# Folding layer norm's sums and the last pairs' key sums with accumulating transfers in a two-layer attention kernel

## The chip, the cores and the metric

The kernel runs on one core of a Trainium2 chip. The metric is the device time of one execution in microseconds (us): 2938.17 before the change, the median of three runs (2936.75 to 2938.68). The profile is of one execution, with a span of 2935.6 us at a mean granted TensorE clock of 0.997.

## The reference

The input x has 8 images of 512 channels and 32 x 32 = 1024 positions, float32. Two attention layers follow each other. Layer 0 normalises each position over its 512 channels, has 8 heads of 64 and adds x. Layer 1 normalises groups of channels and has one head of 512. Cut to what matters:

```python
def _L0_conv_ref(x, Wq, bq, Wk, bk, Wv, bv, Wo, bo, gamma, beta):
    x_flat = x.reshape(B, C, S).transpose(0, 2, 1)
    xn = layer_norm(x_flat, gamma, beta)        # mean and variance over the 512 channels
    q, k, v = ...                               # xn @ W.T + b, 8 heads of 64
    attn = softmax(q k^T / 8)
    return (attn v) @ Wo.T + bo + x_flat

def _L1_conv_ref(x, gamma, beta, wq, bq, wk, bk, wv, bv, wp, bp):
    h = _group_norm(x, gamma, beta)             # 32 groups
    q, k, v = ...                               # w h + b
    attn = softmax(q^T k / sqrt(512))
    return x + wp (v attn^T) + bp
```

So each image needs two sums over channels for each position in layer 0 (of x, and of the squares of x minus its mean), and for each head and query the sum of the exponentials over the keys.

## The kernel before, in words

**Tiling.** Channels or keys lie on the 128 partitions, positions on the free axis. A big tile holds 128 x 1024 float32 (46 of them in one pool), a half tile 128 x 512 (9 of them). A tile of x is a "block": two groups of 128 channels by 512 positions, so that one image is four blocks `xt[j, k]`, j the half of the channels and k the half of the positions. PSUM has three wide tiles (two banks each) and two single banks.

**Products.** Every projection is a blocked product in seven multiplications rather than eight (class `Product`, the list `STEPS`). One step multiplies one block of the left by one block of the right, into an accumulating bank called x, y or z. Some operands are sums of blocks, which VectorE makes: for the right operand they are called T1 to T4 (T1 = 12 - 11, T2 = 22 - T1, T3 = 22 - 12, T4 = 21 - T2), for the left S1 to S4. The third step of a product multiplies S2 and T2. A product is two units (four for layer 1's scores) of seven steps. After its matmuls a step first performs one "tick", then ScalarE or VectorE takes a bank out: a copy `u`, then sums with another bank (line 343).

**Order.** Within `manual_schedule` each engine performs its instructions in the order of the text. Work that may be done beside the matmuls stands in a queue, `side`; a tick performs its first entry, `later(...)` appends, and `until(...)` empties it until a condition holds. Entries of `at_scores` are performed after the fifth score tile of the next pair.

**Layer 0's norm.** `LayerNorm.steps` is a generator whose pieces go through `side`, one at a tick. It adds the blocks of x on VectorE (`lns`, lines 524 and 528), multiplies the sum by a matrix of 1/512 on TensorE (`over_channels`, line 519), which gives the means on 64 partitions of a bank, and has ScalarE copy them to the four quarters of `mu` (line 537). It centres x, squares it on ScalarE, adds the squares (`lnq`) and multiplies again for the variance. `compact` takes 16 columns out of the transposed bank, `inverse_root` finds the root, and `expand` spreads it over a whole tile. The blocks are then scaled. The norm of image b + 1 is queued in `next_values_and_queries`, after the third step of image b's values.

**Layer 0's heads.** A `Pair` is two heads and 512 queries; there are eight for each image. For each of eight blocks of keys TensorE makes scores (line 683), ScalarE the exponentials (line 686), and VectorE adds them up over the blocks (line 692). What is left is a sum over 128 partitions: 64 x 2 keys for each head. For pairs 0 to 5 transfers issued by GpSimd do most of this. `halve` adds the upper 64 partitions to the lower (line 716), `fold` lays 32 partitions over another 32 into a quarter of a half tile (line 713), and `folded_sums` transposes 32 x 32 squares and reduces on VectorE. For pairs 6 and 7 a matmul with ones does it (`product`, line 749), and the last pair's output is multiplied by the inverse sums as it leaves its bank (line 708). The output blocks of those pairs are block 22 of `ot`.

**Layer 1.** `Whole` holds its scores, exponentials, key sums (also folded, in `Whole.fold`) and values. `values` is a product of two units with eight matmul instructions of 512 columns a step; its order is two steps of each unit, then the rest of the first, then the rest of the second. After it come the next image's values and queries.

**What is around.** Loads and stores are issued by SyncE in the order of the text. Weights were saved to DRAM once and are reloaded for each image (`load_w`), and the next image's keys come back as `k_again`.

## Time and profile before

| what | value |
|---|---|
| time, median of 3 | 2938.17 us |
| span of the profile | 2935.6 us, 26956 instructions |
| s matmuls (line 683) and acc matmuls (line 701), busy | 457.1 and 453.6 us |
| ScalarE exponentials (line 686) | 512 of 1050 ns |
| VectorE additions of exponentials (line 692) | 384 of 1225 ns |
| mean matmuls (line 519) | 32 in 8 images, 9.4 us busy |
| variance matmuls (line 519) | 32 in 8 images, 10.6 us busy |
| key sum matmuls of the last pairs (line 749) | 64 in 8 images, 8.5 us busy |
| halving transfers (line 716) | 64 of 256 KB, 3.4 to 7.6 us to landing, median 3.5 |
| folding transfers (line 713) | 256 of 64 KB, 1.8 to 7.4 us to landing, median 2.4 |
| loads of x (line 150) | 32 of 512 KB, 5.3 to 6.8 us to landing, median 6.0 |

A line of the page's groups gives line, engine, operation, output and input tiles with their shapes and count, then busy time and mean duration, then the idle time of the engine before it and what ended it. In a timeline the first number is the start, the second the time from there to the end of the row's last instruction. A float32 matmul of the text appears as two instructions. Matmuls are pipelined, so that the distance of two starts tells what one costs, and its duration is longer.

### The profile page before, as it was taken

How to read it: one execution, taken by the hardware profiler on the slowest of the kernel's cores; microseconds unless marked ns; L12 is line 12 of the kernel's file. 1: busy time of each engine (PE TensorE's matmuls, PEld its weight loads, DVE VectorE, ACT ScalarE, POOL GpSimd, SP SyncE). 2: the span in 40 equal slices, each digit the busy share in tenths (PEclk: the TensorE clock that was granted, in tenths of full speed). 3: DMA queues.
4: the chain of work that ended last, by engine and by line, in shares of the span. 5: the costliest groups of instructions: out<-in, count | busy, mean ns of one | idle time of the engine just before them, and what ended most of it. 6: DMA issues, size and time to landing. Idle time of an engine off the chain costs nothing.

```text
span 2935.6 us, 26956 instructions
## 1 busy us (share of the span) xinstructions
PE 2914.7 (99%) x9787; PEld 1374.3 (47%) x9787; DVE 1788.5 (61%) x2298; ACT 1044.1 (36%) x1641; POOL 238.5 (8%) x357
## 2 busy tenths in 40 slices
PE   9999999999999999999999999999999999999998
PEld 4534455345543455434553345533455334553344
DVE  6677456774567654675557765577555675537744
ACT  3462215612156121651216512264223632226221
POOL 2020000200011000110001100011000100002000
PEclk9999999999999999999999999999999999999999
DMA  8124141231312323132232322322231231412302
GB/s 296 59 47 146 53 136 35 58 138 55 125 39 55 136 66 113 43 83 104 69 111 47 83 101 77 103 52 78 100 112 68 58 107 65 122 33 63 109 4 70
DMA packets 100286, 250.93 MB, mean 85 GB/s; under 512 B 13824, under 2 KB 17968, under 8 KB 100144
## 3 DMA queue, kind: packets, MB, share of 16 engines
q1 hardware_dynamic: 81616, 204.51, 20.4%
q0 software_dynamic: 18432, 44.59, 7.7%
q8 instruction: 79, 1.29, 0.2%
q14 instruction: 63, 0.52, 0.1%
q10 hardware_dynamic: 96, 0.02, 0.0%
HBM read 156.26 MB, written 59.24 MB: 73 GB/s over the span
## 4 chain that ended last, share of the span: by engine, by line
PE 98%; DVE 1%; DMA 0%; issue 0%; ACT 0%; SPq 0%; DVEq 0%
PE s L683 15%; PE acc L701 15%; PE x_o L429 6%; PE x_s L421 6%; PE y_s L421 4%; PE y_o L429 4%; PE z_s L421 4%; PE z_o L429 4%; PE x_q L404 3%; PE x_k L404 3%; PE x_qa L404 3%; PE x_v L413 3%; PE x_vm L413 3%; PE x_out L404 3%; PE y_q L404 2%; PE z_qa L404 2%
## 5 line engine op out<-in xcount | busy, mean ns | idle before, releaser
L686 ACT ACTIVATE p<-s 128x1024 f32<-128x1024 f32 x512 | 476.4, 1050 | 77.3 <-PE s L683 77.2
L692 DVE TENSOR_TENSOR sum<-sum,p 128x1024 f32<-128x1024 f32 x384 | 470.3, 1225 | 38.9 <-ACT p L686 0.9
L701 PE MATMUL acc<-p,v 128*64 128x512 f32 x2048 | 453.6, 595 | 0.0
L683 PE MATMUL s<-q,k_again 64*128 64x512 f32 x1792 | 399.9, 596 | 0.0
L701 PEld LDWEIGHTS acc<-p,v 128*64 128x64 f32 x2048 | 141.4, 137 | 305.0 <-issue 292.2
L683 PEld LDWEIGHTS s<-q,k_again 64*128 64x128 f32 x1792 | 166.3, 185 | 232.0 <-issue 116.1
L716 POOL DMA_DIRECT2D sum<-sum x64 | 54.9, 859 | 2294.9 <-PE z_vm L413 1139.3
L713 POOL DMA_DIRECT2D fold<-sum x256 | 171.2, 764 | 292.5 <-DMA fold<-sum 281.6
L690 DVE TENSOR_TENSOR sum<-p,p 128x1024 f32<-128x1024 f32 x64 | 78.4, 1225 | 190.0 <-ACT p L686 190.0
L421 PE MATMUL x_s<-S_qa,T_gn 128*128 128x512 f32 x256 | 120.3, 592 | 0.0
L429 PE MATMUL x_o<-T_p,S_vm 128*128 128x512 f32 x256 | 115.2, 592 | 0.0
L822 ACT ACTIVATE p<-p 128x512 f32<-128x512 f32 x128 | 80.7, 630 | 73.1 <-DVE p L343 73.1
L705 ACT COPY o<-acc 128x512 f32<-128x512 f32 x56 | 32.8, 586 | 197.4 <-PE acc L701 197.4
L343 DVE TENSOR_TENSOR p<-u(1, 1)_s,y_s 128x512 f32<-128x512 f32 x32 | 22.0, 689 | 132.3 <-ACT u(1, 1)_s L434 132.3
L451 ACT ACTIVATE u(0, 0)_k<-x_k,vecs 128x512 f32<-128x512 f32 x16 | 11.0, 687 | 239.7 <-PE x_k L404 211.0
L343 DVE TENSOR_TENSOR y<-u(1, 1)_o,y_o 128x512 f32<-128x512 f32 x16 | 11.0, 688 | 134.7 <-ACT u(1, 1)_o L434 134.7
L421 PEld LDWEIGHTS x_s<-S_qa,T_gn 128*128 128x128 f32 x256 | 48.6, 190 | 61.2 <-issue 61.0
L429 PEld LDWEIGHTS x_o<-T_p,S_vm 128*128 128x128 f32 x256 | 48.6, 190 | 60.7 <-issue 60.7
L758 ACT COPY rr<-r 32x16 f32<-32x16 f32 x256 | 51.6, 202 | 58.2 <-DVE r L657 55.3
L496 DVE STREAM_TRANSPOSE rden<-rr 128x512 f32<-128x512 f32 (+1 forms) x72 | 51.5, 750 | 26.1 <-ACT rr L878 13.4
L343 DVE TENSOR_TENSOR qa<-u(1, 1)_qa,y_qa 128x512 f32<-128x512 f32 x16 | 11.0, 687 | 82.4 <-ACT u(1, 1)_qa L451 82.4
L413 PE MATMUL x_vm<-w_m,T_gn 128*128 128x256 f32 x256 | 60.5, 379 | 0.0
(327 smaller groups left out, 4541.8 us busy)
## 6 DMA issues: line engine op xcount, KB each, us to landing
x<-in_x_dram SPq DMA_DIRECT2D x32, 512.0 KB, 6.0
sum<-sum POOLq DMA_DIRECT2D x64, 256.0 KB, 3.5
fold<-sum POOLq DMA_DIRECT2D x256, 64.0 KB, 2.4
xr<-in_x_dram SPq DMA_DIRECT2D x64, 256.0 KB, 6.8
x_away<-x SPq DMA_DIRECT2D x32, 512.0 KB
x1r<-x_away SPq DMA_DIRECT2D x64, 256.0 KB, 5.9
out_dram<-y SPq DMA_DIRECT2D x64, 256.0 KB, 2.5
k_away<-k SPq DMA_DIRECT2D x28, 512.0 KB, 2.6
```

Source lines behind the costliest of these rows:

```text
L404: nc.tensor.matmul(dst, a[:, k, ts(r, P)], b[:, k, :], start=(opens and k == 0), stop=(k == 1), skip_group_check=True)
L413: nc.tensor.matmul(dst[:, ts(m, CB)], b[:, k, ts(2 * r + m, P)], a[:, k, :], start=(opens and m == 0 and k == 0), stop=(k == 1), skip_grou ...
L421: nc.tensor.matmul(dst, b[:, k, ts(r, P)], a[:, k, :], start=(opens and k == 0), stop=(k == 1), skip_group_check=True)
L429: nc.tensor.matmul(dst, a[:, m, ts(r, P)], b[m // 2][:, m % 2, :], start=(opens and m == 0), stop=(m == NM // 2 - 1), skip_group_check=True)
L683: nc.tensor.matmul(s[:, ts(i, HB)], self.k[m // 4][r, ts(m % 4, P)], self.q[r, :], start=True, stop=True)
L686: nc.scalar.activation(p, s, AF.Exp, scale=1.0 / float(D) ** 0.5)
L690: nc.vector.tensor_add(self.sum, self.p[0], p)
L692: nc.vector.tensor_add(self.sum, self.sum, p)
L701: nc.tensor.matmul(acc[i * D : (i + 1) * D, :], value_of(self.vt, m, self.c * P + i * D, D), self.p[m][:, ts(i, HB)], start=(m == 0), stop ...
L713: nc.gpsimd.dma_start(out=f[ts(q, BL), :], in_=t[ts(n, BL), cols], accum_op=ALU.add if n else ALU.bypass)
L716: nc.gpsimd.dma_start(out=t[:D, :], in_=t[D:, :], accum_op=ALU.add)
L822: nc.scalar.activation(dest(i, k), dest(i, k), AF.Exp, scale=float(C) ** -0.5)
```

## The change

The aim is to take sums over partitions off TensorE and to let transfers that add do them.

1. **Means.** For images 1 to 7 the sum over channel groups is made by four transfers from DRAM into one tile, the first plain and three adding, issued by GpSimd (`LayerNorm.sums`). `halve` and `fold` follow, and VectorE's `folded_sums` gives the sums, which are spread with eight small ScalarE copies and one transpose (`folded_means`, `spread`). For image b + 2 these sums are issued while image b is at layer 1's values; for image 1 they are issued before image 0's keys.
2. **Variances.** The sum of squares is still added on VectorE, then halved and folded in the same way. Because a transfer takes time, the norm waits between (`waiting`) until the next image's queries begin.
3. **Last pairs.** Pairs 6 and 7 are folded like the others in all images but the last. Their inversion goes through `side` behind three empty entries, and pair 7's output is copied out and scaled afterwards like that of pair 6.
4. **Folds.** A pair's sum is halved and folded as soon as its scores are through (`take`), before the values of the pair ahead, and both first parts of a fold are issued before the two adding parts.
5. **Order.** The norm of image b + 2 is queued within layer 1's values, with x loaded there; the weights of the queries are loaded after them; the query product has one tick a step instead of two.

```diff
-LN_AT = 3
...
+    def fold(f, q, t):
+
+        for n in range(2):
+            for i in range(NH):
+                nc.gpsimd.dma_start(out=f[ts(q + i, BL), :], in_=t[ts(n, BL), ts(i, HB)],
+                                    accum_op=ALU.add if n else ALU.bypass)
...
     class LayerNorm:
...
+        def sums(self):
+
+            self.total = big_tile(f"lns_{self.b}")
+            for c in range(NC):
+                nc.gpsimd.dma_start(out=self.total, in_=x[self.b, ts(c, P), :],
+                                    accum_op=ALU.add if c else ALU.bypass)
+            self.fold("mu")
...
+        def fold(self, name):
+            self.f = half_tile(f"fold_{name}_{self.b}")
+            halve(self.total)
+            fold(self.f, 0, self.total)
+
+        def folded_means(self, name):
+
+            d = small.tile([P, HB // BL], F32, tag=f"ln{name}", name=f"ln{name}_{self.b}")
+            t = half_tile(f"fold{name}_{self.b}")
+            folded_sums(d[:D, :], t[:D, :], self.f[:D, :])
+            nc.vector.tensor_scalar(d[:D, :], d[:D, :], 1.0 / C, None, ALU.mult)
+            return d
+
+        def spread(self, name, r):
+            rr = small.tile([P, NH, HB // BL], F32, tag=f"ln{name}r", name=f"ln{name}r_{self.b}")
+            for j in range(4):
+                for k in range(NH):
+                    nc.scalar.copy(rr[ts(j, BL), k, :], r[ts(k, BL), :])
+            yield
+            t = big_tile(f"{name}_{self.b}")
+            setattr(self, name, t)
+            expand(t, rr.rearrange("p k i -> p (k i)"))
+            yield
...
         def steps(self):
...
-            for k in range(NH):
-                yield from self.add("lns", k, self.xt[0, k], self.xt[1, k])
-            yield
-            self.mean()
-            yield
-            yield
+            if self.folded:
+                yield from self.spread("mu", self.folded_means("m"))
+            else:
...
-            yield
-            self.variance()
-            yield
-            yield from self.root()
+            if self.folded:
+                self.fold("var")
+                yield
+                while self.waiting:
+                    yield
+                yield from self.root_folded()
+            else:
...
+        def take(self, pair):
+
+            n = len(self.two)
+            self.two.append(pair)
+            if self.folded:
+                if n == 0:
+                    self.f = half_tile(f"fold_{self.tag}")
                 halve(pair.sum)
-            for n, pair in enumerate(self.two):
-                for i in range(2):
-                    fold(self.f, 2 * n + i, pair.sum, ts(i, HB))
+                fold(self.f, 2 * n, pair.sum)
...
+        ln = LayerNorm(1)
+        ln.sums()
+        ln.xt = load_x(1)
         units, kt = project("k0", wk_now, bias_of("bk0"), hb)
...
             units, q = project(f"q{b}", wq, bias_of("bq0"), hb, True)
-            for u in units:
-                u.pieces = 2
+            units[0].step(0 if b else 6)
+            if ln:
+                ln.waiting = False
             units[0].rest()
...
-                p.values(scaled=(p is pairs[-1]))
...
+                p.values(scaled=(i == HEADS - 1 and not more))
+                sums = groups[i // 2]
...
+                elif i % 2 == 1 and sums.folded:
+                    if i + 1 < HEADS:
+                        at_scores.append(sums.invert_folded)
                     else:
-                        sums.product()
-                        later(sums.invert, sums.copies, lambda: sums.rows(1), lambda: sums.rows(0),
-                              lambda: sums.scale(0))
-                elif i + 1 < len(pairs):
-                    at_scores.append(sums.invert_folded)
+                        later(*(nothing,) * 3, sums.invert_folded)
                     later(sums.copies, *(lambda s=sums, f=f, n=n: f(s, n) for f in (PairSums.rows, PairSums.scale)
                                          for n in range(2)))
...
             if more:
-                wv_next, wq_next = load_w("v", b + 1), load_w("q", b + 1)
+                wv_next = load_w("v", b + 1)
             o_units = whole.values(vm)
             check = iter(()) if more else all_checks()
             o_units[0].step(1)
+            ln = LayerNorm(b + 2) if b + 2 < B else None
+            if ln:
+                ln.sums()
             whole.inverse()
             o_units[0].step(1)
             next(check, None)
             o_units[1].step(2)
             next(check, None)
-            for u in o_units:
-                u.rest()
-            until(lambda: not side)
+            o_units[0].rest()
+            if ln:
+                ln.xt = load_x(b + 2)
+                ln.queue()
+            o_units[1].rest()
+            if more:
+                wq_next = load_w("q", b + 1)
```

## The prediction

> **What bounds the kernel now.** I read the page from its head: busy time, the clock in the slices, the chain that ended last.

> ```profile
> PE 2914.7 (99%) x9787; PEld 1374.3 (47%) x9787; DVE 1788.5 (61%) x2298; ACT 1044.1 (36%) x1641; POOL 238.5 (8%) x357
> PEclk9999999999999999999999999999999999999999
> PE 98%; DVE 1%; DMA 0%; issue 0%; ACT 0%; SPq 0%; DVEq 0%
> ```

> TensorE is busy in all but 21 us of 2935.6, at full clock, and the chain is made of it. So a matmul taken out of its queue is time taken off the end, unless another engine then makes TensorE wait. Next, what TensorE waited for: 13 us in all, nearly all single waits at the kernel's start and in its last image. No stage repeats a wait, so little can be gained from waits; the price list is what each removed matmul takes in the stream. The timeline of TensorE round the mean, the variance and the last pairs' key sums, for the fifth image's norm and for the fourth image's last pairs:

> ```profile
> 1524.76 1.89 PE L413 MATMUL z_v<-w_v,x 128*128 128x256 f32 x8
> 1526.58 1.08 PE L519 MATMUL mean<-lns,ones_c 128*64 128x512 f32 x4
> 1527.59 1.99 PE L413 MATMUL x_v<-w_v,T_h 128*128 128x256 f32 x8
> 1529.42 1.89 PE L413 MATMUL y_v<-w_v,T_h 128*128 128x256 f32 x8
> ...
> 1541.48 1.88 PE L404 MATMUL y_q<-T_h,w_q 128*128 128x512 f32 x4
> 1543.29 1.08 PE L519 MATMUL var<-lnq,ones_c 128*64 128x512 f32 x4
> 1544.30 1.98 PE L404 MATMUL x_q<-T_h,w_q 128*128 128x512 f32 x4
> 1546.12 1.88 PE L404 MATMUL z_q<-T_h,w_q 128*128 128x512 f32 x4
> ...
> 1309.50 1.07 PE L749 MATMUL den<-sum,ones 128*32 128x512 f32 x8
> 1310.50 7.09 PE L701 MATMUL acc<-p,v 128*64 128x512 f32 x32
> ```

> Durations overlap, so I take starts. A step of v follows the next at 1.73 us (y_v to the following x_v: 1531.15 - 1529.42), so two steps should take 3.45; from z_v to y_v it is 4.66: the mean costs 1.21 us. For q a step is 1.72, two 3.43; from y_q to z_q 4.64: the variance costs 1.21. The key sums cost 1310.50 - 1309.50 = 1.00.

> [...] (512 KB weight saves land in 3.1 us at the fastest) [...] 256 KB add in 3.5. [...] 281.6 us of idle time before the fold transfers end with a fold landing. [...]

> **Part 1, off TensorE.** Images 1 to 7 lose mean and variance matmuls, images 0 to 6 the last pairs' product: 7 x (1.21 + 1.21 + 1.00) = 23.9 us, all on the path. Image 0's norm and image 7's product stay.

> **Part 2, the last pairs' scaling.** Their fold starts when pair 7's sum is done. Before, that sum ended at 1309.4. Halving 3.8 (3.5 and the wait) and two rounds of folds, 3.2 each, give 1319.8; the inversion now comes at the k projection's fourth step, after VectorE's addition ends at 1322.4 (1321.4 with TensorE 1.0 earlier). Hidden, by 1.6 us, behind k's first unit. But scale(0) and scale(1) now fall into the ticks of out's first two steps, which pushes T1 and T2 of o back by a tick. The same stage before:

> ```profile
> 1331.60 0.75 DVE L783 SCALAR_TENSOR_TENSOR u(0, 0)_out<-x_out,bo,xr 128x512 f32<-128x512 f32 x1 [1.03 <-PE x_out L404]
> 1332.27 1.22 DVE L483 TENSOR_TENSOR T_o<-o,o 128x1024 f32<-128x1024 f32 x1
> 1333.40 0.68 DVE L343 TENSOR_TENSOR x<-u(0, 0)_out,z_out 128x512 f32<-128x512 f32 x1
> 1334.00 1.22 DVE L483 TENSOR_TENSOR T_o<-o,T_o 128x1024 f32<-128x1024 f32 x1
> 1335.14 0.75 DVE L783 SCALAR_TENSOR_TENSOR u(0, 0)_out<-x_out,bo,xr 128x512 f32<-128x512 f32 x1
> ```

> With the new order a scaling (0.69) stands where T1 stood at 1332.27, T1 where T2 stood at 1334.00, and T2 comes after the x_out addition of the second unit, at 1335.80, and ends at 1336.95. TensorE wants T2 for its fifth out step, which started at 1336.55: a stall of 0.5 us, 7 times, **+3.5 us**. Bounds: none (0), or a whole tick (1.7 us, 12 in all).

> **Part 3, sums of x from DRAM.** Per image 1 to 7: four 512 KB transfers into one tile, chained; one halving; four folds in two rounds. No row shows a 512 KB add. From above: 3.1 us (a plain save) at the least, 7.6 (the slowest halving) at the most. The estimate: from 64 KB (2.4) to 256 KB (3.5) is 1.1 us for 192 KB, so 512 KB is 5.0; with wait and issue 5.3. Chain: 4 x 5.3 + 3.8 + 6.4 (two rounds of folds) = 31.4 us.

> When does it start? In the loop it is issued after the first two steps of layer 1's values in the text, but GpSimd runs ahead: its last fold for layer 1's key sums was issued at 1460.5, and the new order of these folds is no longer. The tile needs a free big buffer; the last to come free is one of the value projection's operands, at 1462.9. I take 1462: the sums are ready at 1493.4.

> When are they needed? At the tick of the second value unit's third step. VectorE gets there when the first unit's last addition ends, 1496.2. So no wait on a DMA, with 2.8 us in hand. Then VectorE: transpose 0.7, reduce 0.7, multiply 0.2, to 1497.8. ScalarE: eight copies (1.7, as the pairs' eight do), to 1499.5; queued behind them, the copy u(0, 1) of that step, 0.6, to 1500.2. TensorE wants it for the fifth step, which started at 1500.65. It just fits: +0.

> VectorE beside it: the two wide and two half additions of x go (2 x 1.22 + 2 x 0.69 = 3.8 us per image), transpose, reduce and the spread of the mean (1.25) come (2.9). The centring moves up into the last value steps and delays the next v additions by some 2 us; the banks that they free are wanted later than that. No cost. ScalarE loses four 0.58 copies. Nothing here is on the path.

> **Part 4, variances.** Halve and fold, 10.2 us, after the last sum of squares: the seventh tick of v's first unit, about 1522.5, so ready at 1533; read at q's first step, 1535. Hidden, behind v's second unit. Image 1: the sums start at about 40 us, beside the loads of the start, and are read at 86: hidden, though the saves of the weights queue behind them and free their buffers 15 to 20 us later.

> **Part 5, moved loads.** x, 2 MB, now issued at 1496.7 and landing 6 us later (6.0 median), before the centring that follows two ticks after the mean; w_q after the last store, 1513.7, for use at 1536. Hidden. The traffic grows by 7 x 2.1 MB = 15 MB on 251, at DMA shares of 1 to 4 tenths.

> Sum: -23.9 + 3.5 = -20.4; 2938.2 - 20.4 = 2917.8.

> **The rivals.**
> A, the forecast: 2918, with T2's stall; spread 2914 to 2921. Chance 0.58.
> B, the delayed T2 costs nothing, because the scalings run in gaps of VectorE: 2938.2 - 23.9 = 2914. For it: VectorE is 61% busy. Against: the listing shows VectorE without a gap of 0.1 us from 1331.6 to the end of T2. 0.10.
> C, the means come late. VectorE waits in its queue, ScalarE's copies behind it, and TensorE for u(0, 1). With 7.6 + 0.3 us a transfer the chain is 31.6 + 3.8 + 6.4 = 41.8, to 1503.8; plus 1.6 + 1.7 + 0.6 = 1507.7, against 1500.65: 7 us in each of six images, 42 in all: 2960, slower. Against: few loads run in that window once x and w_q are moved. For: a margin of 2.8 us is thin, and the adding rate from DRAM is not shown. 0.23, of which 0.06 still gain 6 us or more, 0.06 land within 6 us of before and 0.11 are slower.
> D, buffers: in the first image saves and sums share GpSimd's queue and x takes four tiles early; a fold's tile is held longer in the pool of nine half tiles. One or two stalls, 2 to 10 us: 2920 to 2928. 0.09.

> **How the numbers follow.** Faster by over 0.2% (5.9 us): A, B, D and a quarter of C, 0.83. Same: 0.06. Slower: 0.11. The range leaves out C's far side and the edges: from B's 2914 less 2 us for waits that vanish too, to 2930, the mild side of C.

> **What would show it.** TensorE's instructions fall by 7 x (4 + 4 + 8) = 112 to 9675; line 519's matmuls remain 8 in all, the key sum product 8. TensorE waits 7 times some 0.5 us for T_o. If the means are in time, VectorE's transpose of the folded means waits for no DMA; if rival C holds, it waits for "fold" and TensorE for ScalarE's u(0, 1)_o, in six places. A time over 2932 would mean that some wait of 2 us or more per image took the matmuls' place; one under 2912 that a removed matmul cost more than its slot.

## The result and the profile after

The changed kernel takes 2947.74 us (median of 4) beside 2937.6 of the kernel before (median of 4, a fourth run beside the three known before): ratio 1.0035, 95% interval 1.0018 to 1.0052. It is slower by 10 us, where 20 us less were forecast.

The page of the changed kernel, in the order in which the one before was read: busy time, clock, chain. PE is TensorE and PEld its loading of weights, DVE is VectorE, ACT ScalarE, POOL GpSimd and SP SyncE; a q behind the name stands for the engine's instruction queue.

```profile
PE 2901.9 (98%) x9675; PEld 1374.4 (47%) x9675; DVE 1790.7 (61%) x2307; ACT 1054.5 (36%) x1732; POOL 363.1 (12%) x525
PEclk9999999999999999999999999999999999999999
PE 85%; DVE 6%; DMA 5%; ACT 2%; issue 2%; POOL 0%; SPq 0%; DVEq 0%; POOLq 0%; ACTq 0%
```

112 matmul instructions are gone, as forecast. But TensorE's idle time rose from 20.9 to 45.6 us, and the chain is no longer TensorE alone: 13% of it is VectorE, transfers and ScalarE. What TensorE waited for, in the view of waits (us in total, times, longest), cut to what is new:

```profile
PE y_k L403 <- DVE k L342: 17.2, 7, 2.7
...
PE x_q L403 <- ACT u(0, 1)_q L450: 3.5, 7, 1.1
...
PE x_out L403 <- DVE T_o L482: 1.9, 7, 0.3
PE y_v L412 <- DVE v L342: 1.3, 4, 0.3
```

One wait stands out: once for each of images 0 to 6, the last step of the next k projection's first unit waits about 2.5 us for VectorE. That is the sign that the prediction named for a time over 2932, a wait of 2 us or more per image in the matmuls' place. The timeline of TensorE there, for the fourth image; a bracket gives the engine's idle time before the row and what ended it:

```profile
1328.34 1.88 PE L403 MATMUL x_k<-T_h,w_k 128*128 128x512 f32 x4
1330.06 1.88 PE L403 MATMUL z_k<-T_h,w_k 128*128 128x512 f32 x4
1334.61 3.18 PE L403 MATMUL y_k<-x,w_k 128*128 128x512 f32 x4 [2.67 <-DVE k L342]
1337.58 2.43 PE L403 MATMUL x_out<-o,w_o 128*128 128x512 f32 x4
1339.84 1.88 PE L403 MATMUL z_out<-o,w_o 128*128 128x512 f32 x4
```

A step's row lasts 1.88 us and the next starts 1.72 after it (x_k to z_k). So from z_k to z_out, three steps, it should be 5.15 us; it is 9.78. The wait is only part of it: y_k and x_out are themselves slow. The busy times by stretch show why. A row gives the stretch, its length and the busy time and instructions of PE, PEld, DVE, ACT and POOL; then come the granted clock, the DMA engines' share and GB/s:

```profile
1330.00:1334.60 4.60, 1.94 (x5) 0.57 (x3) 2.19 (x7) 2.88 (x10) 0.00 (x0) 1.00 0.18 57
1334.60:1336.00 1.40, 1.39 (x3) 0.64 (x4) 1.40 (x3) 0.00 (x0) 0.00 (x0) 0.73 0.21 57
1336.00:1338.00 2.00, 2.00 (x4) 0.89 (x3) 0.54 (x2) 0.00 (x0) 0.00 (x0) 0.50 0.24 91
1338.00:1340.00 2.00, 2.00 (x5) 0.85 (x4) 1.12 (x2) 0.00 (x0) 0.00 (x0) 0.83 0.00 0
```

After the wait the clock is halved for 3.4 us (in the trace's clock record from 1335.26 to 1338.67); the 40 slices of the page, each 74 us long, don't show it. Over the seven images the excess from z_k to z_out is 4.34, 2.58, 4.25, 4.63, 2.52, 4.47 and 2.99 us, 25.8 in all.

Now the cause, from the timelines of VectorE, ScalarE, GpSimd and SyncE.

```profile
1329.62 0.71 DVE L509 STREAM_TRANSPOSE foldt<-fold 128x512 f32<-128x512 f32 x1 [3.75 <-DMA fold<-sum]
...
1333.87 0.69 DVE L342 TENSOR_TENSOR k<-u(1, 1)_k,y_k 128x512 f32<-128x512 f32 x1 [2.31 <-ACT u(1, 1)_k L450]
```

```profile
1331.43 1.69 ACT L813 COPY rr<-r 32x16 f32<-32x16 f32 x8 [3.92 <-DVE r L723]
1333.15 0.69 ACT L450 ACTIVATE u(1, 1)_k<-x_k,vecs 128x512 f32<-128x512 f32 x1
```

```profile
1314.98 0.80 POOL L505 DMA_DIRECT2D sum<-sum  x1 [6.58 <-PE acc L767]
1318.70 1.06 POOL L501 DMA_DIRECT2D fold<-sum  x2 [2.92 <-DMA sum<-sum]
1326.28 1.62 POOL L501 DMA_DIRECT2D fold<-sum  x2 [6.52 <-DMA fold<-sum]
```

```profile
1316.84 0.33 SPq L837 DMA_DIRECT2D xr<-in_x_dram  x1
1317.27 2.11 SPq L203 DMA_DIRECT2D w_a<-saved_a  x4
```

Read from the bottom. SyncE issues the reload of w_a, 1.8 MB, from 1317.27. GpSimd issues the last pair's first fold parts at 1318.70, 64 KB each; the second parts, which wait for them, are issued only at 1326.28. VectorE stands at the inversion's transpose until 1329.62. ScalarE's eight copies wait for it, and u(1, 1)_k stands behind them in ScalarE's queue and starts at 1333.15, though its bank was full by about 1330.2, when TensorE had gone on to z_k. VectorE's addition of y_k waits for that copy, and TensorE, which must add into that bank again in y_k, waits for the addition.

The account: 23.9 off, 25.8 for these stops, 7 x 0.43 = 3.0 for T_o, some 4.6 for u(0, 1)_q and 1.9 for y_v (waits, and some 0.15 us of restart each), and 1.0 more for single waits in the first image (var, pst_k): +12.4 us. The spans of the two profiles differ by 11.9, the medians by 10.1.

### The profile page after: what moved, and what is told of

The parts are those of the page before. It is cut to its first block, busy times and chain, and to the rows that moved or that the text cites. A ratio compares the mean times of both kernels' runs of the same rounds, so it can differ in the third digit from the quotient of the medians.

```text
span 2947.5 us, 27096 instructions
## 1 busy us (share of the span) xinstructions
PE 2901.9 (98%) x9675; PEld 1374.4 (47%) x9675; DVE 1790.7 (61%) x2307; ACT 1054.5 (36%) x1732; POOL 363.1 (12%) x525
## 4 chain that ended last, share of the span: by engine, by line
PE 85%; DVE 6%; DMA 5%; ACT 2%; issue 2%; POOL 0%; SPq 0%; DVEq 0%; POOLq 0%; ACTq 0%
PE s L749 13%; PE acc L767 11%; PE x_o L428 6%; PE x_s L420 6%; PE y_s L420 4%; PE z_s L420 4%; PE y_o L428 3%; PE z_o L428 3%; PE x_qa L403 3%; PE x_vm L412 3%; DMA fold<-sum 3%; PE x_out L403 3%; PE x_q L403 3%; PE x_v L412 2%; PE y_qa L403 2%; PE y_vm L412 2%
## 5 line engine op out<-in xcount | busy, mean ns | idle before, releaser
L749 PE MATMUL s<-q,k_again 64*128 64x512 f32 x1792 | 399.7, 596 | 0.0
L749 PEld LDWEIGHTS s<-q,k_again 64*128 64x128 f32 x1792 | 166.6, 185 | 231.4 <-issue 116.1
L505 POOL DMA_DIRECT2D sum<-sum x78 | 63.1, 809 | 1670.3 <-PE z_vm L412 993.0
L501 POOL DMA_DIRECT2D fold<-sum x312 | 207.2, 746 | 383.8 <-DMA sum<-sum 162.4
L963 DVE SCALAR_TENSOR_TENSOR y<-y,bm,x1r 128x512 f32<-128x512 f32 x64 | 48.1, 752 | 52.0 <-DMA x1r<-x_away 50.4
L403 PE MATMUL x_out<-T_o,w_o 128*128 128x512 f32 x128 | 60.9, 598 | 1.9 <-DVE T_o L482 1.9
L495 DVE STREAM_TRANSPOSE rden<-rr 128x512 f32<-128x512 f32 (+1 forms) x72 | 52.2, 751 | 14.0 <-ACT rr L935 12.4
```

The source lines that it names most:

```text
L403: nc.tensor.matmul(dst, a[:, k, ts(r, P)], b[:, k, :], start=(opens and k == 0), stop=(k == 1), skip_group_check=True)
L501: nc.gpsimd.dma_start(out=f[ts(q + i, BL), :], in_=t[ts(n, BL), ts(i, HB)], accum_op=ALU.add if n else ALU.bypass)
L505: nc.gpsimd.dma_start(out=t[:D, :], in_=t[D:, :], accum_op=ALU.add)
L749: nc.tensor.matmul(s[:, ts(i, HB)], self.k[m // 4][r, ts(m % 4, P)], self.q[r, :], start=True, stop=True)
```

## The experiments

The theory: w_a's reload holds up the last fold, three engines wait in turn, and TensorE's clock falls after some of the stops. Rivals: the fold's chain is too long wherever w_a is loaded; the layer norm's part costs the gain; the slow matmuls have another cause than idle time. Times are medians; the ratios are to the kernel before on the same chip.

| kernel | us | before | ratio, 95% interval |
|---|---|---|---|
| e1_product_back | 2926.83 | 2936.18 | 0.9967, 0.9953 to 0.9982 |
| e2_wa_late | 2925.29 | 2936.18 | 0.9964, 0.9951 to 0.9976 |
| e4_pairs_only | 2952.03 | 2936.18 | 1.0055, 1.0039 to 1.0072 |
| e3_all_three | 2920.22 | 2936.18 | 0.9945, 0.9928 to 0.9961 |
| e3_again | 2917.68 | 2936.11 | 0.9935, 0.9918 to 0.9951 |
| e5_filler | 2940.21 | 2936.11 | 1.0015, 1.0006 to 1.0023 |
| e7_half_wa | 2931.08 | 2936.11 | 0.9981, 0.9973 to 0.9989 |
| e6_norm_two_ticks_later | 2945.48 | 2936.11 | 1.0037, 1.0023 to 1.0052 |
| e8_loads_behind_x1r | 2912.28 | 2936.52 | 0.9917, 0.9903 to 0.9930 |

### e1_product_back: the last pairs by the matmul again

```diff
-                groups.append(PairSums(f"{b}_{i // 2}", more or i + 2 < HEADS))
+                groups.append(PairSums(f"{b}_{i // 2}", i + 2 < HEADS))
...
-                p.values(scaled=(i == HEADS - 1 and not more))
+                p.values(scaled=(i == HEADS - 1))
```

> The changed kernel with one part undone: the last pairs' key sums of every image come from the matmul with ones again, and pair 7 is scaled as it leaves its bank. Theory (the reload of w_a holds up the last fold; VectorE, ScalarE and then the k projection's seventh step wait for it, and TensorE's clock halves after some of these stops): the seven stops, 25.8 us in the profile with the slow matmuls behind them, and the seven waits for T_o, 3.0 us, go, the product's 7.0 us come back: 2947.7 - 28.8 + 7.0 = 2926 us. Rival (the layer norm's part eats the gain, by its waits for u(0, 1)_q and by moved loads): 2938 or more.

2926.8 us. The wait of y_k is gone. So the layer norm's part alone makes the kernel faster, by 9.4 us. It takes 7 x 2.42 = 16.9 off TensorE; the 7.5 us between are about what its own waits come to (x_q 3.2, y_out 1.8, y_v 1.6 in the view of waits, and some 2 for 15 restarts).

### e4_pairs_only: the last pairs' fold alone

The norm's sums by transfers are left unused; the norm is queued and x and w_q are loaded as in the kernel before.

```diff
-        ln = LayerNorm(1)
-        ln.sums()
-        ln.xt = load_x(1)
...
+                ln = LayerNorm(b + 1, False)
+                ln.xt = xt
+                ln.queue()
```

> One part alone: the folding of the last pairs' key sums, with pairs folded as soon as they are through, as in the changed kernel, but all layer norms by matmuls, with x and w_q loaded, the norm queued and the ticks counted as in the kernel before. Theory: 2937.6 - 7.0 for the product + 25.8 for the stops + 3.0 for T_o = 2959 us. Rival (the layer norm's part is what costs): 2931 to 2938.

2952.0 us: slower by 15.9 us, so the loss lies in this part. It was forecast at 2959; the stops were somewhat shorter here. The seven waits of y_k sum to 14.9 us, not 17.2, and in the first image no slow matmuls follow (y_k at 252.44, x_out at 254.26); the clock halved after three of the stops, not four.

### e2_wa_late: w_a loaded behind the output projection

```diff
-            wa_now = load_w("a", b)
             ob = operands(ot)
...
+            wa_now = load_w("a", b)
             wm_now = load_w("m", b)
```

> The changed kernel with the four loads of w_a moved in the text from ahead of the output projection to behind it, so that they are issued after the last fold has landed. Theory (w_a's 1.8 MB fill the DMA engines while the last fold's first parts are under way): the fold's first parts land in 2.5 to 3.5 us instead of 7, no wait of y_k for VectorE, 2947.7 - 25.8 = 2922 us. Rival (the last fold's own chain of halving, two rounds, inversion and eight copies is too long for the place of its inversion, whatever is loaded beside it): the wait of y_k stays at 1.5 us or more in each image, 2935 us or more.

2925.3 us: 10.9 us faster than the kernel before, where the changed kernel was 10.1 us slower, with nothing but four loads moved. GpSimd's timeline at the last fold of the fourth image:

```profile
1304.27 0.80 POOL L505 DMA_DIRECT2D sum<-sum  x1 [6.64 <-DVE sum L758]
1308.02 1.06 POOL L501 DMA_DIRECT2D fold<-sum  x2 [2.95 <-DMA sum<-sum]
1310.17 1.62 POOL L501 DMA_DIRECT2D fold<-sum  x2 [1.09 <-DMA fold<-sum]
```

The second parts follow the first 2.15 us later instead of 7.58, and the view of waits has no y_k. The chain itself fits; the rival that it is too long falls. So does the thought that VectorE's work beside the fold slows it: from 1308 to 1310 VectorE is busy for 2.00 of 2 us here too.

### e7_half_wa: half of the load

```diff
-            wa_now = load_w("a", b)
+            wa_now = weight_tiles(f"a_{b}")
+            for g in range(2):
+                d, t = saved_part("a", wa_now, g)
+                nc.sync.dma_start(out=t, in_=d)
...
+            for g in range(2, 4):
+                d, t = saved_part("a", wa_now, g)
+                nc.sync.dma_start(out=t, in_=d)
             wm_now = load_w("m", b)
```

> The changed kernel with two of w_a's four loads (0.8 of 1.8 MB) moved behind the output projection, the first two left where they are. Theory (the fold's first parts wait for as many bytes as lie ahead of them): 1.0 MB at the 350 GB/s of that stretch takes 3.0 us instead of 5.2, so the first parts land 2 us or more earlier, 4.5 to 5 us after their issue instead of 7, and y_k's wait falls from 2.5 us to under 0.6; 2922 to 2929 us. Rival (any large load beside a fold costs the same): the wait stays above 1.5 us, 2938 us or more.

2931.1 us, between the two, a little more than the theory gave. GpSimd's timeline there:

```profile
1308.70 1.06 POOL L501 DMA_DIRECT2D fold<-sum  x2 [2.95 <-DMA sum<-sum]
1314.20 1.61 POOL L501 DMA_DIRECT2D fold<-sum  x2 [4.44 <-DMA fold<-sum]
```

From first to second parts: 2.15 us with none of w_a ahead, 5.50 with 1.0 MB, 7.58 with 1.8 MB. At the 350 GB/s that the changed kernel's transfers reached from 1320 to 1322 the whole load takes 5.2 us, by estimate, and the fold is later by 5.4. The wait of y_k falls to 4.6 us in seven images. The rival (any large load costs the same) falls. The theory holds in size, though the fold does not wait for all of the bytes ahead of it (last section).

### e5_filler: TensorE kept busy during the stop

```diff
-                k_units[0].rest()
+                k_units[0].step(6)
+                ps = wide_psum(f"filler_{b}")
+                for _ in range(3):
+                    nc.tensor.matmul(ps[:, :HB], wk_next["11"][:, 0, :P], hb["11"][:, 0, :], start=True, stop=True)
+                k_units[0].rest()
```

> The changed kernel with three matmuls of 128x512 more (2.6 us) ahead of the seventh step of the k projection's first unit in images 0 to 6, on operands that lie ready, into a wide PSUM tile that nothing reads; they fill TensorE's wait for VectorE without changing when that wait ends. Theory (the stop is a wait of some 2.5 us, and the slow matmuls behind it come from TensorE's clock, which is halved after an idle stretch): the wait becomes 0.3 us or less, y_k and x_out run at 1.72 us a step in every image, and of the 25.8 us only the 7.3 us beyond the bare waits are saved: 2940 us. Rival (the slow matmuls come from what runs beside them, the transposes and loads): y_k still takes up to 3.6 us in some images, 2947 to 2949 us.

2940.2 us with 21 matmuls more than the changed kernel: 4.1 us slower than the kernel before instead of 10.1, for more work. TensorE's timeline in the first image:

```profile
247.14 1.88 PE L403 MATMUL z_k<-T_h,w_k 128*128 128x512 f32 x4
248.86 2.74 PE L1108 MATMUL filler<-x,w_k 128*128 128x512 f32 x6
251.43 1.88 PE L403 MATMUL y_k<-x,w_k 128*128 128x512 f32 x4
253.15 1.88 PE L403 MATMUL x_out<-o,w_o 128*128 128x512 f32 x4
```

y_k follows the fillers without a wait, and the next step comes after 1.72 us. The transposes, transfers and late fold are all still there (VectorE waits 23.5 us in seven images for the fold), and the clock record has no halving between the first 60 us and the last image, so the slow matmuls came from the idle stretch.

### e3_all_three: w_a late, the inversion one tick earlier, ScalarE's copies apart

```diff
-                        later(*(nothing,) * 3, sums.invert_folded)
+                        later(*(nothing,) * 2, sums.invert_folded)
...
             refine()
+            yield
             yield from self.spread("rstd", r)
```

(and the edit of e2_wa_late)

> The changed kernel with three edits: w_a's loads behind the output projection as in e2_wa_late; two empty entries instead of three ahead of the last pairs' inversion, so that the scalings are through one step earlier and T1 and T2 of o come where they came before; and one more yield between the norm's refinement and its eight copies, so that u(0, 1)_q isn't queued behind them. Theory: the 25.8 us of the stops, the 3.0 us for T_o and some 3.5 us for u(0, 1)_q all go: 2947.7 - 32.3 = 2915 us, better than both kernels. Rival (the fold comes too late for an inversion one step earlier): a wait at the k projection's steps of 1 us or more in each image, 2922 us or more.

> e3_all_three once more, beside e6_norm_two_ticks_later on one chip: the same 2920 us if nothing differs from the first time.

2920.2 us and, in another comparison, 2917.7 (the intervals of the two ratios overlap): faster than both kernels, though not the 2915 expected. The waits for T_o are gone and that for u(0, 1)_q is left once, in the first image. New in the view of waits, as in e2_wa_late:

```profile
PE z_v L412 <- DVE v L342: 3.7, 6, 0.9
...
PE y_v L412 <- DVE v L342: 2.0, 6, 0.3
```

### e6_norm_two_ticks_later: the centring moved into v

```diff
                 ln.xt = load_x(b + 2)
+                later(nothing, nothing)
                 ln.queue()
...
-            units[0].step(0 if b else 6)
+            units[0].step(2 if b else 6)
```

> e3_all_three with two empty entries ahead of the norm's pieces in layer 1's values, so that the centring falls into the v projection and no longer between the last additions of layer 1, and with the norm's second half released two steps later in the q projection. Theory (what is left over from the forecast is VectorE's backlog at the start of v, where the last additions wait for x1r and the centring stands ahead of v's additions): the 5.7 us that z_v and y_v wait for VectorE, with their restarts some 7 us, go: 2913 us. Rival (the backlog moves with the pieces, or the variances now come too late for q): 2920 us or more, with waits of TensorE in v or q.

2945.5 us: this attempt failed, and the rival's words fit. ScalarE's timeline:

```profile
1519.17 2.19 ACT L604 ACTIVATE sq<-x 128x1024 f32<-128x1024 f32 x2 [4.62 <-DVE x L600]
1521.27 0.57 ACT L433 COPY u(0, 1)_v<-x_v 128x512 f32<-128x512 f32 x1
```

Squares of x, which wait for VectorE's centring, now stand ahead of the copy u(0, 1)_v, and TensorE waits for that copy, 17.8 us in six images. The order of VectorE was eased and that of ScalarE made worse. The five runs go from 2939.6 (the one profiled) to 2952.3 us, as their mean granted clocks go from 0.996 to 0.992; 0.004 of 2945 us is 11.8 of these 12.7.

### e8_loads_behind_x1r: w_q and k_again behind the last x1r

VectorE's timeline in e3_all_three shows what heads the backlog at the start of v:

```profile
1507.92 0.75 DVE L964 SCALAR_TENSOR_TENSOR y<-y,bm,x1r 128x512 f32<-128x512 f32 x1 [3.10 <-DMA x1r<-x_away]
1508.59 1.22 DVE L600 TENSOR_TENSOR x<-x,mu 128x1024 f32<-128x1024 f32 x1
```

and SyncE's timeline of the same stretch has w_q's first two loads at 1498.99, ahead of that x1r at 1502.78.

```diff
-            if more:
-                wq_next = load_w("q", b + 1)
...
-            for u in units:
-                u.rest()
+            units[0].rest()
+            wq = loads() or wq
+            units[1].rest()
```

(`loads` issues w_q and the four k_again)

> e3_all_three with the loads of w_q and k_again moved in the text behind the first unit of the next image's values, so that they are issued after the last loads of x1r and not ahead of them. Theory (what is left is the same mechanism once more: the last x1r transfers stand behind w_q's 1.8 MB, VectorE waits for them up to 3 us with the centring and v's additions behind, and TensorE's z_v and y_v wait for those): the waits of z_v and y_v, 5.7 us with some 2 us of restarts, go: 2910 to 2914 us where e3_all_three has 2918 to 2920. Rival (the centring itself is the backlog): the waits of z_v stay and the time is that of e3_all_three. A second rival (w_q or k_again now come late): new waits of x_q or s for a DMA, slower than e3_all_three.

2912.3 us, 0.9917 of the kernel before, with no wait of z_v or y_v left and no new one for a DMA in v, q or the scores, so both rivals fall. VectorE's wait at the same place falls from 3.10 to 1.30 us. What TensorE still waits for is, but for the first image's u(0, 1)_q and some tenths in single waits, what it waited for before the change.

## Why the prediction was wrong

**Failed: part 2, "Hidden, by 1.6 us, behind k's first unit".** The term "two rounds of folds, 3.2 each" was mis-sized: the first round took 7.58 us. The other terms of the chain held: 3.72 us for the halving where 3.8 was taken, 3.34 for the second round, and VectorE came to the inversion 11.4 us after the sum where 12.0 was taken. (The sum 1309.4 + 3.8 + 6.4 is 1319.6, not 1319.8; that changes nothing.) So a fold forecast 1.6 us early came 3.75 us late. I took a typical fold, though the row that I had gives 1.8 to 7.4 us, and I did not ask what else is loaded there. The trace before had it. The stretch in which the new fold would fly, in the kernel before:

```profile
1311.00:1313.00 2.00, 2.00 (x12) 0.70 (x10) 1.88 (x6) 0.18 (x1) 0.00 (x0) 1.00 0.28 87
1313.00:1315.00 2.00, 2.00 (x12) 0.72 (x10) 0.46 (x1) 1.43 (x8) 0.00 (x0) 1.00 0.98 312
1315.00:1317.00 2.00, 2.00 (x14) 0.57 (x8) 1.97 (x4) 0.00 (x0) 0.00 (x0) 1.00 0.92 322
```

A DMA share of 0.98 and 0.92: w_a and xr filled all engines just when the fold would want them. It cost nothing there because nothing on the path waited for a transfer. With a margin of 1.6 us and a chain of three transfers, that view decides. e2_wa_late and e7_half_wa show it by size, e4_pairs_only by part.

**Failed with it: the bounds.** I carried both ends of the transfer times for the means (rival C), not for the pairs' fold, so no rival named this stop. My rivals put the risk on the means, and none of them came about: T2's stall was there (against B), the means were in time (against C), and the first image's single waits grew by only 1.0 us (D).

**Missed: the clock.** I counted a wait as its own length. In four of seven images the excess is 1.9 us beyond the wait, in the other three 0.3, so that the half clock cost some 1.7 us each, half of the 3.4 us that it lasts; e5_filler gives it back. The kernel before shows the same in its last image, where TensorE waits for the group norm:

```profile
2776.00:2778.00 2.00, 0.59 (x2) 0.50 (x2) 0.65 (x5) 0.47 (x2) 0.00 (x0) 0.50 0.20 78
2778.00:2780.00 2.00, 0.35 (x1) 0.35 (x2) 1.86 (x7) 1.21 (x2) 0.00 (x0) 0.50 0.00 0
2780.00:2782.00 2.00, 2.00 (x3) 0.83 (x3) 2.00 (x5) 0.31 (x1) 0.00 (x0) 0.50 0.00 0
```

**Right: part 1.** 9675 instructions, and where nothing else intrudes the steps close up: in the changed kernel, from z_v to y_v without the mean,

```profile
1534.24 1.89 PE L412 MATMUL z_v<-w_v,x 128*128 128x256 f32 x8
1535.96 1.89 PE L412 MATMUL x_v<-w_v,T_h 128*128 128x256 f32 x8
1537.69 1.89 PE L412 MATMUL y_v<-w_v,T_h 128*128 128x256 f32 x8
```

3.45 us where it was 4.66. e8_loads_behind_x1r, without the waits, is 24.2 us faster than the kernel before, and 23.9 were counted.

**Right: T_o.** 0.28 us of wait and 0.43 with the restart, where 0.5 was taken. With the inversion one tick earlier (e3_all_three) it goes.

**Right by two errors: part 3.** No transpose of the folded means waits for a transfer. By luck: the sums started at 1465.4, 5.5 us sooner against TensorE than assumed (layer 1's values start 8.9 us later than before); each transfer took 4.2 to 5.8 us against the 5.3 estimated; and the halving took 8.4 us instead of 3.8. x's own 2 MB, issued by SyncE from 1482.99 and not, as I had it from the text, behind the first unit's stores, was issued just ahead of it. The early start (5.5 us) paid for a chain some 5 us longer than the 31.4 forecast.

**Missed: part 4 and the moved loads.** For the variances, "Hidden, behind v's second unit" held for VectorE but not for the eight copies behind them on ScalarE, which stand ahead of u(0, 1)_q: 0.5 us an image, gone in all but the first with e3_all_three's extra yield. And the loads of w_q, also put down as hidden, delayed x1r: visible once the larger stop was gone (e3_all_three), and shown by e8_loads_behind_x1r. The traffic grew by 29.4 MB (280.3 against 250.9), not 15: I counted x's reads from DRAM but not the new halvings and folds.

## What to carry to other kernels

A small transfer that takes a matmul's place on the way to TensorE's next step must be priced with what is loaded beside it at that time: look at the DMA share of that very stretch in the kernel before, not at the median row. Then move the bulk loads that have time out of its way; here that, with two small changes of order, turned 10 us lost into 24 us gained, and no arithmetic was changed. And a wait of TensorE costs more than its length when the clock falls after it (here by some 1.7 us, after about 2 us idle within one stretch of 3.41 us); where instructions queue in order, ask what stands behind each new wait on all engines, not only on the one that waits.

## What the runs showed of the hardware

**A small transfer behind the bulk loads of another queue waited for a part of them, then shared the engines with the rest.** From the issue of the fold's first parts to that of its second, the seven images have 2.14 to 2.16 us with none of w_a ahead (e2_wa_late), 5.37 to 5.94 with 1.0 MB (e7_half_wa) and 7.17 to 7.62 with 1.8 MB (the changed kernel); 0.25 MB of xr stand ahead in all three. The parts are issued 1.4 to 1.5 us after w_a's first load, and just ahead of its fourth. The queues of the changed kernel, q1 SyncE's and q0 GpSimd's, with records, MB and share of the 16 engines, from 1320 to 1322.5 and then from 1322.5 to 1325.7:

```profile
q1 hardware_dynamic: 244, 0.88, 101.1%
...
q1 hardware_dynamic: 268, 0.71, 69.8%
q0 software_dynamic: 63, 0.13, 12.3%
```

So the fold, issued at 1318.70, moves nothing until 1322.5, and then its 0.13 MB move among w_a's. Over the images its first record starts 3.9 to 4.1 us after the issue, where e7_half_wa has 3.0 to 3.4 and e2_wa_late 1.1. Against e2_wa_late the first record of the changed kernel is late by 2.8 to 3.0 us, by estimate about 1.0 MB at the 350 GB/s from 1320 to 1322. Why the fold's records start just there no run shows.

```profile
253.23:256.64 3.41, 1.34 (x3) 0.68 (x4) 2.08 (x4) 1.82 (x5) 0.00 (x0) 1.00 0.09 26
256.64:260.06 3.42, 3.42 (x5) 1.35 (x4) 1.70 (x3) 0.00 (x0) 0.00 (x0) 0.50 0.14 52
...
611.63:615.04 3.41, 1.42 (x4) 0.35 (x2) 1.03 (x5) 2.75 (x10) 0.00 (x0) 1.00 0.25 77
615.04:618.45 3.41, 3.08 (x7) 1.44 (x8) 3.15 (x6) 0.13 (x1) 0.00 (x0) 1.00 0.22 77
...
2410.45:2413.87 3.42, 2.07 (x5) 0.57 (x3) 1.63 (x5) 1.71 (x9) 0.00 (x0) 1.00 0.24 77
2413.87:2417.28 3.41, 2.04 (x5) 1.06 (x6) 2.52 (x5) 1.17 (x2) 0.00 (x0) 1.00 0.22 76
```

The longest stop, 2.72 us, is cut in two by the grid and costs 0.3 us beyond its length; a shorter one, of which 2.07 us fall into one stretch, halves the clock in the next. TensorE was busy for 1.34, 1.18, 0.74 and 1.09 us in the stretches ahead of the four halvings, and for 1.42 us or more in those without. In all eleven traces, past the first 60 us, no stretch at full clock with up to 1.82 us idle was followed by a halving and each with 2.07 or more was; between them one of 1.95 was and one of 1.99, that from 611.63 above, was not (matmul ends are modelled). So a stretch need not be idle throughout: about 2 us of its 3.41 were enough here.
